# Key slices of the first two blocks stored from the query pool's tiles, x transposed in pairs, second context split sooner

## The chip, the core and the metric

The kernel runs on one core of one Trainium2 chip. The metric is the device time of one execution in microseconds. TensorE multiplies, ScalarE, VectorE and GpSimd do the elementwise work, SyncE issues nearly all DMA transfers. Each engine works through its own instructions in order and waits on semaphores for the others.

## The reference

The input `x` has 32 sequences of 100 tokens with 512 features. One layer is computed in float32: a cross-attention against a second input, the context, with a causal mask, and a mixture-of-experts feed-forward.

```python
q = (layernorm(x) @ WQ.T)      # 16 heads of 32
k = ctx @ WK.T
v = ctx @ WV.T
scores = q @ k.T / sqrt(32), causal mask     # per sequence and head
x = x + (softmax(scores) @ v) @ Wfc.T + bfc
h = layernorm(x)
# each of 16 experts picks 12 tokens of every sequence by its softmax score
x = x + sum over experts of gelu(h@Wg.T) * (h@Wu.T) @ Wd.T * weight + shared expert(h)
```

The mask lets a query see only keys up to its own position, so just the first 100 context tokens of each sequence take part.

## The kernel before

Every large product is computed from two parts of each operand. A helper copies a tile to a rounded high part on ScalarE (`split`, L101, or L135 in `ctx_split`) and subtracts it from the original on VectorE or GpSimd for the low part (L102, L136). `mm3` (L56) then issues three matmuls for each of four 128-feature slices: high by high, low by high, high by low. All projections go to PSUM tiles named `kv`, of which there are two (`pj=2`).

The 3200 context tokens are cut into nine blocks of two or three times 128 tokens (`KVB`). For each block, `kproj(j, c)` computes one of four key slices (`c`, 128 features), `kkeep` copies it to an SBUF tile `kk` on ScalarE (L204) and stores it to the DRAM tensor `kD` (L205). `vproj` and `vkeep` do the same for values (tile `vt`, two of them, L187, tensor `vD`). The pool of `kk` has two tiles of 384 columns, the pool of the query tiles `q` three of 400 columns:

```python
BUF = dict(cr=4, raw=6, cx=8, x=4, v=2, kk=2, kt=2, vt=2, q=3, p=5, pt=5, y=2, pj=2, sc=1, tr=2)
```

A tile of a pool can be written again only when everything that reads it, a DMA store included, is done. Keys come back from `kD` per unit of work (`kload`, L210). The x rows of a batch of four sequences are loaded (`x_load`), measured (`x_stats`: VectorE, then two small GpSimd instructions for `rs`, L152 and L153), normalized (`x_norm`, L159), and transposed by `x_turn`: four TensorE transposes (L171) into one of two PSUM tiles `ms`, then a ScalarE cast `xnh` (L101) and a VectorE subtract `xnl` (L102), which frees the `ms` tile. Queries come from `qproj` and `qkeep` (L230).

`prologue()` fills this pipeline. It handles context blocks 0 and 1 whole and prepares block 2; then the loop over 32 units (four feature slices for each of eight batches) runs scores (L240), softmax (L251 to L275), turned probabilities (L281, L286) and values (L296), with the remaining context blocks mixed in. After it come the feed-forward groups and the experts. In the prologue and the units the order of instructions on all engines is the order in which the code is written, so a line that stands earlier in `prologue()` is issued earlier on each engine that it uses. SyncE likewise issues the loads and stores in that order: the load of `x(1, 0)`, which reuses the tile of x block (0, 0), stands ahead of the store of the second value tile, the first key store of block 1, and `kload(0)`.

Of the kernel before, what the change touches and what calls it, by code (L numbers as in the profile page):

```python
# [7 lines left out]
F32 = mybir.dt.float32  # L8
# [13 lines left out]
SB = T // NSB  # L22
# [4 lines left out]
KMAX = 384  # L27
# [13 lines left out]
def f32(ap):  # L41
    return ap.bitcast(F32)
# [18 lines left out]
def attention(tc, K, F):  # L61
    nc = tc.nc
    with ExitStack() as ctx, ExitStack() as kvctx:
        def pool(name, bufs, stack=ctx, **kw):
            return stack.enter_context(tc.tile_pool(name=name, bufs=bufs, **kw))
# [4 lines left out]
        qp = pool("a_q", BUF["q"])  # L70
# [10 lines left out]
        kkp = pool("a_kk", BUF["kk"], kvctx, side="right")  # L81
# [22 lines left out]
        def load_w(w, dk):  # L104
            r = raw.tile([128, D], F32, name="raw")
            nc.sync.dma_start(r, K.wA[w, :, dk, :])
            return r

        def split_w(w, dk, r):
            split(WH[w][:, dk, :], WL[w][:, dk, :], r)  # L110

        def load_wc(w, c):
            r = raw.tile([128, D], F32, name="raw")
            nc.sync.dma_start(r.rearrange("p (d n) -> p d n", d=NC4),
                              K.wA[w, :, :, c * 128:(c + 1) * 128])
            return r

        def split_wc(w, c, r, eng=None):
            cs = slice(c * 128, (c + 1) * 128)
            split(WH[w][:, :, cs], WL[w][:, :, cs], r.rearrange("p (d n) -> p d n", d=NC4), eng)  # L120
# [3 lines left out]
        def ctx_load(j, d):  # L124
            t0, n = KSTART[j] * 128, KVB[j] * 128
            cr = crp.tile([128, KMAX], F32, name="cr")
            nc.sync.dma_start(cr[:, 0:n], K.ctxT[d, :, t0:t0 + n])
            cur["cr", j, d] = cr

        def ctx_split(j, d, eng=nc.gpsimd):  # L130
            n = KVB[j] * 128
            cr = cur.pop(("cr", j, d))
            h = cxp.tile([128, KMAX], FR, name="cxh")
            l = cxp.tile([128, KMAX], FR, name="cxl")
            nc.scalar.copy(h[:, 0:n], cr[:, 0:n])  # L135
            eng.tensor_tensor(l[:, 0:n], cr[:, 0:n], f32(h[:, 0:n]), ALU.subtract)  # L136
            cur.setdefault(("ch", j), []).append(h)
            cur.setdefault(("cl", j), []).append(l)

        def x_load(sb, b):  # L140
            xt = xp.tile([S, D], F32, name="xt")
            r0 = (sb * 4 + b) * S
            nc.sync.dma_start(xt, K.x[r0:r0 + S, :])
            cur["x", sb, b] = xt

        def x_stats(sb, b):
            st = stp.tile([S, 6], F32, name="bst")
            mv = stp.tile([S, 2], F32, name="mv")
            rs = stp.tile([S, 1], F32, name="rs")
            nc.vector.bn_stats(st, cur["x", sb, b])  # L150
            nc.vector.bn_aggr(mv, st)
            nc.gpsimd.tensor_scalar(rs, mv[:, 1:2], EPS, None, ALU.add)  # L152
            nc.gpsimd.tensor_tensor(rs, rs, K.nhalf[0:S, 0:1], ALU.pow)  # L153
            cur["mv", sb, b] = mv, rs

        def x_norm(sb, b):
            xt = cur["x", sb, b]
            mv, rs = cur["mv", sb, b]
            nc.vector.tensor_scalar(xt, xt, mv[:, 0:1], rs, ALU.subtract, ALU.mult)  # L159
# [16 lines left out]
        def vproj(j, i):  # L176
            ps = ps_kv.tile([128, D], F32, name="kv")
            cs = slice(i * 128, (i + 1) * 128)
            ch, cl = cur["ch", j], cur["cl", j]
            mm3(nc, ps, [((ch[d][:, cs], cl[d][:, cs]),  # L180
                          (WH[1][:, d, :], WL[1][:, d, :])) for d in range(NC4)],
                by_term=(j == 0))
            return ps

        def vkeep(j, i, ps):
            v = vtp.tile([128, D], F32, name="vt")
            nc.scalar.copy(v, ps)  # L187
            t0 = (KSTART[j] + i) * 128
            nc.sync.dma_start(K.vD[t0:t0 + 128, :], v)

        def kproj(j, c):
            n = KVB[j] * 128
            cs = slice(c * 128, (c + 1) * 128)
            ch, cl = cur["ch", j], cur["cl", j]
            pk = ps_kv.tile([128, D], F32, name="kv")
            mm3(nc, pk[:, 0:n], [((WH[0][:, d, cs], WL[0][:, d, cs]),
                                  (ch[d][:, 0:n], cl[d][:, 0:n])) for d in range(NC4)],
                by_term=(j == 0))
            return pk

        def kkeep(j, c, pk):
            t0, n = KSTART[j] * 128, KVB[j] * 128
            kk = kkp.tile([128, KMAX], F32, name="kk")
            nc.scalar.copy(kk[:, 0:n], pk[:, 0:n])  # L204
            nc.sync.dma_start(K.kD[:, c, t0:t0 + n], kk[:, 0:n])  # L205

        def kload(u):
            sb, c = divmod(u, NC4)
            kt = ktp.tile([128, SB], F32, name="kt")
            nc.sync.dma_start(kt, K.kD[:, c, sb * SB:(sb + 1) * SB])  # L210
            cur["k", u] = kt
# [99 lines left out]
        def prologue():  # L311
            nc.gpsimd.dma_start(mask, K.mask)
            z = stp.tile([128, 128], F32, name="zero")
            nc.vector.memset(z, 0.0)
            zp = ps_ms.tile([128, NC4, 128], F32, name="ms")
            for _ in range(WARM):
                nc.tensor.matmul(zp[:, 0, :], z, z, start=True, stop=True)
            wk = [load_wc(0, 0)]
            for d in range(NC4):
                ctx_load(0, d)  # L320
            wk += [load_wc(0, c) for c in range(1, NC4)]
            wv = [load_w(1, 0), load_w(1, 1)]
            split_wc(0, 0, wk[0])
            for d in range(NC4):
                ctx_split(0, d, nc.vector)
            wv.append(load_w(1, 2))
            for b in range(2):
                x_load(0, b)
            p0 = kproj(0, 0)
            split_wc(0, 1, wk[1])  # L330
            wv.append(load_w(1, 3))
            kkeep(0, 0, p0)
            p0 = kproj(0, 1)
            split_wc(0, 2, wk[2])
            split_wc(0, 3, wk[3])
            for b in range(2, 4):
                x_load(0, b)
            for d in range(NC4):
                ctx_load(1, d)
            wq = [load_wc(2, 0), load_wc(2, 1)]  # L340
            kkeep(0, 1, p0)
            p0 = kproj(0, 2)
            split_w(1, 0, wv[0])
            split_w(1, 1, wv[1])
            kkeep(0, 2, p0)
            p0 = kproj(0, 3)
            split_w(1, 2, wv[2])
            x_stats(0, 0)
            split_w(1, 3, wv[3])
            wq += [load_wc(2, 2), load_wc(2, 3)]  # L350
            kkeep(0, 3, p0)
            p0 = vproj(0, 0)
            x_norm(0, 0)
            x_stats(0, 1)
            x_stats(0, 2)
            x_norm(0, 1)
            x_stats(0, 3)
            for d in range(NC4):
                ctx_split(1, d, nc.vector)
            x_norm(0, 2)  # L360
            x_norm(0, 3)
            vkeep(0, 0, p0)
            p0 = vproj(0, 1)
            split_wc(2, 0, wq[0])
            for d in range(NC4):
                ctx_load(2, d)
            x_load(1, 0)
            vkeep(0, 1, p0)
            for c in range(NC4):
                kkeep(1, c, kproj(1, c))  # L370
                if c == 0:
                    for b in range(4):
                        x_turn(0, b)
                if c:
                    split_wc(2, c, wq[c], nc.gpsimd)
                    ctx_split(2, c - 1)
                else:
                    kload(0)
            x_load(1, 1)
            ctx_load(3, 0)  # L380
            x_stats(1, 0)
            vkeep(1, 0, vproj(1, 0))
            x_norm(1, 0)
# [153 lines left out]

        with tc.manual_schedule(engines={mybir.EngineType.Pool}):
            prologue()
            for u in range(NU - 3):  # L540
                sb, c = divmod(u, NC4)
# [3 lines left out]
                j, ck = divmod(u - KS, NC4)  # L545
# [784 lines left out]
```

## Time and profile before

| quantity | value |
|---|---|
| time, median of 3 runs | 1678.12 us (1677.43 to 1681.89) |
| profiled execution, its own time | 1681.51 us |
| profiled execution, span | 1679.6 us |
| mean granted TensorE clock | 0.997 |
| TensorE busy | 1660.7 us (99%) |
| ScalarE, VectorE, GpSimd busy | 679.2, 920.8, 625.2 us |
| mean DMA rate over the span | 141 GB/s |

A row of a profile view names the line of the code, the engine, the operation and `out<-in` by the program's tile names. "Idle before" is the time that the engine stood still just ahead of an instruction, with the instruction or transfer that ended it. The clock column is the share of full TensorE speed that was granted.

### The profile page before, as it was taken

The page shows a single profiled execution, that of the slowest core. Times are in us where ns is not written, and L with a number is a line of the kernel's source. Part 1 is how long each engine was busy: PE and PEld are TensorE (multiplying, and loading weights), DVE is VectorE, ACT ScalarE, POOL GpSimd, SP SyncE. Part 2 cuts the span into 40 slices and gives each one's busy share as a digit, 9 for nine tenths or more (in the row PEclk, how much of TensorE's full clock was granted, in tenths as well). Part 3 has the DMA queues.
Part 4 walks back from the last instruction along what each step waited for, and adds up shares of the span by engine and source line. Part 5 has one row for each costly group of instructions (what it writes and reads, how often), then busy time and mean ns, then how long its engine had stood idle before and what let it go on. Part 6 is the DMA issues. An engine that isn't in the chain of part 4 may idle for free.

```text
span 1679.6 us, 28091 instructions
## 1 busy us (share of the span) xinstructions
PE 1660.7 (99%) x10879; PEld 1526.4 (91%) x10879; DVE 920.8 (55%) x2199; ACT 679.2 (40%) x1088; POOL 625.2 (37%) x542
## 2 busy tenths in 40 slices
PE   8999999999999999999999999999999999999998
PEld 7998888879889898989899999999999999999998
DVE  4778777665433434343555555555555555555542
ACT  4556555553111111112334444444444444444442
POOL 2778777680110011010243344333344333344011
PEclk9999999999999999999999999999999999999999
DMA  7456554556312223211445554455555455555452
GB/s 214 145 171 189 159 159 142 172 191 196 103 66 90 76 82 132 82 44 42 144 163 152 166 169 145 157 161 146 166 167 151 155 161 155 159 161 159 136 165 63
DMA packets 107126, 237.47 MB, mean 141 GB/s; under 512 B 14162, under 2 KB 58419, under 8 KB 106993
## 3 DMA queue, kind: packets, MB, share of 16 engines
q1 hardware_dynamic: 93632, 209.99, 38.3%
q0 software_dynamic: 12944, 25.22, 7.9%
q8 instruction: 85, 1.39, 0.3%
q10 hardware_dynamic: 416, 0.48, 0.1%
q14 instruction: 49, 0.39, 0.1%
HBM read 181.90 MB, written 53.73 MB: 140 GB/s over the span
## 4 chain that ended last, share of the span: by engine, by line
PE 93%; DVE 2%; ACT 1%; POOL 1%; DMA 1%; issue 1%; SPq 0%; ACTq 0%; POOLq 0%; DVEq 0%
PE gu L56 49%; PE dn L56 24%; PE kv L56 10%; PE m L56 3%; PE ms L281 2%; PE ms L296 2%; POOL p L260 1%; PE sc L240 1%; DVE p L251 1%; DMA kD<-kk 1%; ACT pt L286 1%; PE ms L171 0%; DVE y L102 0%; PE m L1109 0%; DMA raw<-wA 0%
## 5 line engine op out<-in xcount | busy, mean ns | idle before, releaser
L56 PE MATMUL gu<-xh,whl 128*128 128x384 f32 (+1 forms) x3200 | 642.5, 332 | 0.0
L56 PEld LDWEIGHTS gu<-xh,whl 128*128 128x128 f32 x3200 | 556.5, 188 | 20.0 <-issue 1.3
L56 PE MATMUL dn<-whl,hh 128*128 128x512 f32 x1168 | 365.9, 394 | 0.0
L740 DVE TENSOR_TENSOR whl<-wraw,whl 128x1536 fp32r<-128x1536 f32 x142 | 249.7, 1759 | 203.2 <-ACT whl L739 181.6
L945 POOL DMA_INDIRECT gx<-xnD,iq x180 | 226.8, 1260 | 359.9 <-DVE big L976 300.3
L56 PE MATMUL gu<-xl,whl 128*128 128x384 f32 (+1 forms) x1600 | 336.7, 332 | 0.0
L56 PEld LDWEIGHTS gu<-xl,whl 128*128 128x128 f32 x1600 | 279.9, 188 | 0.0
L774 ACT CAST hh<-g 128x384 fp32r<-128x384 f32 (+1 forms) x200 | 100.9, 505 | 408.8 <-DVE g L771 380.4
L771 DVE TENSOR_TENSOR g<-g,gu 128x384 f32<-128x384 f32 (+1 forms) x200 | 108.3, 542 | 255.5 <-PE gu L56 249.1
L56 PEld LDWEIGHTS dn<-whl,hh 128*128 128x128 f32 x1168 | 215.6, 188 | 35.8
L739 ACT CAST whl<-wraw 128x1536 fp32r<-128x1536 f32 x142 | 210.0, 1479 | 61.8 <-PE dn L56 58.7
L56 PE MATMUL dn<-whl,hl 128*128 128x512 f32 x584 | 230.6, 395 | 0.0
L770 ACT ACTIVATE g<-gu 128x384 f32<-128x384 f32 (+1 forms) x200 | 96.3, 482 | 237.6 <-PE gu L56 236.9
L775 DVE TENSOR_TENSOR hl<-g,hh 128x384 fp32r<-128x384 f32 (+1 forms) x200 | 113.3, 566 | 114.2 <-ACT hh L774 113.7
L988 POOL DMA_INDIRECT out_dram<-x,isl x48 | 77.8, 1620 | 171.3 <-ACT x L987 161.5
L56 PEld LDWEIGHTS dn<-whl,hl 128*128 128x128 f32 x584 | 109.7, 188 | 25.2
L260 POOL TENSOR_TENSOR p<-p,mx 100x800 f32<-100x800 f32 x64 | 96.7, 1531 | 64.4 <-DVE mx L251 61.4
L275 POOL TENSOR_TENSOR p<-p,sm 100x800 f32<-100x800 f32 x64 | 100.9, 1577 | 5.8 <-DVE sm L270 3.6
L251 DVE CUSTOM_DVE_ANT_0 p<-sc,mask 100x100 f32<-100x100 f32 x512 | 95.4, 256 | 0.0
L1025 POOL TENSOR_TENSOR x<-x,bfc 128x512 f32<-128x512 f32 x23 | 30.9, 1369 | 154.2 <-DMA x<-x 154.2
L977 ACT CAST xh<-big 128x512 fp32r<-128x512 f32 x59 | 36.6, 621 | 101.6 <-DVE big L976 101.6
L269 DVE TENSOR_REDUCE sm<-p 100x8 f32<-100x800 f32 x64 | 63.1, 986 | 24.6 <-ACT p L264 24.6
(160 smaller groups left out, 1645.1 us busy)
## 6 DMA issues: line engine op xcount, KB each, us to landing
wraw<-wE SPq DMA_DIRECT2D x144, 768.0 KB
yD<-y SPq DMA_DIRECT2D x31, 400.0 KB
xt<-x SPq DMA_DIRECT2D x32, 200.0 KB
vD<-vt SPq DMA_DIRECT2D x25, 256.0 KB
kt<-kD SPq DMA_DIRECT2D x32, 200.0 KB
v<-vD SPq DMA_DIRECT2D x8, 800.0 KB
xnD<-xn SPq DMA_DIRECT2D x25, 256.0 KB
out_dram<-x SPq DMA_DIRECT2D x25, 256.0 KB
```

What stands on the lines that cost most here:

```text
L56: r = nc.tensor.matmul(out, t[0][a], t[1][b], start=(first and i == 0), stop=(last and i == n - 1))
L251: nc.vector.tensor_tensor_reduce(out=p[:, bb, h, :], in0=sc[:, h, cs], in1=mask, scale=ISCALE, scalar=NEG, op0=ALU.add, op1=ALU.max, accum ...
L260: nc.gpsimd.tensor_tensor(pv, pv, mx[:, :, None].to_broadcast([S, 8, S]), ALU.subtract)
L275: nc.gpsimd.tensor_tensor(pv, pv, sm[:, :, None].to_broadcast([S, 8, S]), ALU.mult)
L739: nc.scalar.copy(h, r)
L740: nc.vector.tensor_tensor(l, r, f32(h), ALU.subtract)
L770: nc.scalar.activation(g[:, 0:t], pg[:, 0:t], AF.Gelu)
L771: nc.vector.tensor_tensor(g[:, 0:t], g[:, 0:t], pu[:, 0:t], ALU.mult)
L774: nc.scalar.copy(hh[:, 0:t], g[:, 0:t])
L775: nc.vector.tensor_tensor(hl[:, 0:t], g[:, 0:t], f32(hh[:, 0:t]), ALU.subtract)
L945: nc.gpsimd.indirect_dma_start(out=g[:, k, :], out_offset=None, in_=self.K.xn.rearrange("t (a f) -> (t a) f", f=128), in_offset=bass.Indir ...
L988: ins = nc.gpsimd.indirect_dma_start(out=self.K.out, out_offset=bass.IndirectOffsetOnAxis(ap=r.isl[:, i:i + 1], axis=0), in_=o, in_offset= ...
```

## The change

Three edits, all in the attention's start. First, `kkeep` takes its tile from the query pool for the third and fourth key slice of blocks 0 and 1. Second, the four `x_turn` calls of the first batch, which followed the first key slice of block 1 together, are issued two after the second slice and two after the third. Third, in `prologue()` the four splits of context block 1 move ahead of the norm of x block 1 and of the statistics of x blocks 2 and 3.

```diff
         def kkeep(j, c, pk):
             t0, n = KSTART[j] * 128, KVB[j] * 128
-            kk = kkp.tile([128, KMAX], F32, name="kk")
+            if j < 2 and c > 1:
+                kk = qp.tile([128, SB], F32, name="q")
+            else:
+                kk = kkp.tile([128, KMAX], F32, name="kk")
             nc.scalar.copy(kk[:, 0:n], pk[:, 0:n])
             nc.sync.dma_start(K.kD[:, c, t0:t0 + n], kk[:, 0:n])
...
             p0 = vproj(0, 0)
             x_norm(0, 0)
             x_stats(0, 1)
-            x_stats(0, 2)
-            x_norm(0, 1)
-            x_stats(0, 3)
             for d in range(NC4):
                 ctx_split(1, d, nc.vector)
+            x_norm(0, 1)
+            x_stats(0, 2)
+            x_stats(0, 3)
             x_norm(0, 2)
             x_norm(0, 3)
             vkeep(0, 0, p0)
...
             for c in range(NC4):
                 kkeep(1, c, kproj(1, c))
-                if c == 0:
-                    for b in range(4):
+                if c in (1, 2):
+                    for b in (2 * c - 2, 2 * c - 1):
                         x_turn(0, b)
                 if c:
                     split_wc(2, c, wq[c], nc.gpsimd)
```

## The prediction

> **What bounds the kernel now.** I read the page first (engines and slices), then who waits for whom on TensorE, then TensorE and ScalarE in order of time for 15 to 43 us, the chain of waits there, and the windows with the granted clock. The page says that TensorE is the bound; only its idle time or slow clock can be won.
>
> ```profile
> PE 1660.7 (99%) x10879; PEld 1526.4 (91%) x10879; DVE 920.8 (55%) x2199; ACT 679.2 (40%) x1088; POOL 625.2 (37%) x542
> ```
>
> TensorE's waits in the first 400 us, in the form "waiter <- releaser: us in total, times, longest":
>
> ```profile
> PE ms L296 <- ACT pt L286: 3.3, 4, 2.3
> PE kv L56 <- ACT kk L204: 3.1, 2, 2.0
> PE ms L281 <- ACT pt L286: 2.0, 2, 1.6
> ...
> PE ms L171 <- DVE xnl L102: 0.8, 1, 0.8
> ```
>
> The second and last row lie in the prologue, which the change edits. TensorE and then ScalarE in order of time (start, us, instruction, idle before it and its releaser):
>
> ```profile
> 16.63 0.49 PE L56 MATMUL kv<-wh,cxh 128*128 128x512 f32 x1 [1.16 <-ACT kk L204]
> ...
> 21.98 0.50 PE L56 MATMUL kv<-wh,cxh 128*128 128x512 f32 x1 [1.96 <-ACT kk L204]
> ...
> 29.54 1.05 PE L171 MATMUL ms<-ident,xt 100*128 100x100 f32 x8 [0.85 <-DVE xnl L102]
> ...
> 34.76 1.09 PE L56 MATMUL kv<-wh,cxh 128*128 128x512 f32 x4
> ```
> ```profile
> 16.20 0.37 ACT L204 COPY kk<-kv 128x256 f32<-128x256 f32 x1 [2.77 <-DMA kD<-kk]
> ...
> 21.56 0.37 ACT L204 COPY kk<-kv 128x256 f32<-128x256 f32 x1 [3.94 <-DMA kD<-kk]
> ```
>
> ScalarE can't copy the third key slice out of PSUM before the first one's store has left its `kk` tile, nor the fourth before the second's. The PSUM tiles `kv` number two, so TensorE stops at the first value projection until the third slice is out (16.63) and at the second until the fourth is out (21.98). The chain of waits has the two stores:
>
> ```profile
> 10.06 6.04 DMA kD<-kk
> ...
> 17.16 4.30 DMA kD<-kk
> ```
>
> The stops also cost clock. Windows of 2 us: TensorE busy after the first comma; the granted clock, the DMA share and GB/s are the last three numbers.
>
> ```profile
> 20.00:22.00 2.00, 0.04 (x2) 0.02 (x1) 1.91 (x4) 0.44 (x2) 0.43 (x2) 1.00 1.01 298
> 22.00:24.00 2.00, 2.00 (x8) 1.65 (x9) 1.75 (x5) 2.00 (x6) 1.44 (x4) 0.87 0.35 110
> 24.00:26.00 2.00, 2.00 (x6) 1.56 (x5) 2.00 (x7) 0.16 (x1) 0.77 (x2) 0.50 0.69 213
> 26.00:28.00 2.00, 2.00 (x15) 1.98 (x14) 0.61 (x2) 0.59 (x1) 0.00 (x0) 0.78 0.91 292
> 28.00:30.00 2.00, 1.15 (x13) 0.87 (x10) 1.06 (x2) 1.19 (x3) 0.00 (x0) 1.00 0.31 75
> 30.00:32.00 2.00, 2.00 (x19) 1.98 (x18) 1.33 (x3) 0.98 (x2) 0.00 (x0) 1.00 0.71 244
> ```
>
> From 0.87, 0.50 and 0.78 the clock was halved for 0.52 + 2.00 + 0.88 = 3.4 us, from 23.48 to 26.88, after 2.1 us without matmuls.
>
> **The change part by part.** My measure is the start of the block-1 value projection `vproj(1, 0)`, 34.76 before: from there TensorE runs without a gap over 0.2 us up to 168 us.
>
> *Key slices in `q` tiles.* Four copies and four stores stay what they are (copy 0.37 us, 128 KB); only the tile is another. The first and second slices of block 0 keep `kk`. In the forecast the third copy follows its projection. The row of matmuls of 256 columns has a pitch of 0.12 us and starts its last one at 15.19; the third slice's last one is 12 matmuls earlier, 13.75, and ends 0.28 later at 14.03, so the copy runs 14.1 to 14.5 instead of 16.20. Then ScalarE casts the third and fourth value-weight quarter. The fourth lands at 15.77 (the trace's completion events), so its cast ends at 16.4 and the fourth slice's copy at 16.7 instead of 21.9. TensorE: `vproj(0, 0)` starts at 15.31, one pitch after 15.19, and takes 12 x 0.2325 = 2.79 (its quarters are split by 15.7 and 17.1, needed at 16.9 and 17.6); `vproj(0, 1)` from 18.1 to 20.9, since its PSUM tile is free from 16.7.
>
> *Second context split sooner.* No instruction is added. The context quarters land at 18.4 to 19.6 and ScalarE's casts, no longer behind the fourth copy, end at 20.0. VectorE's four subtracts at 0.42 then end at 20.7. In the old order two statistics (0.69 + 0.18 each) and a norm (0.55) stand before them; these now come after, so the norms of x blocks 1, 2 and 3 end near 21.2, 23.4 and 24.3. Cover: TensorE's transposes of them come at 24.1, 25.9 and 26.2. If it were gone, they would cost their excess, at most the 2.3 us that were moved. GpSimd's order is the same; between the small rs steps and its first weight part it sat idle 8.25 us (25 to 33).
> `kproj(1, 0)` can then start at 20.9: the first value copy frees its PSUM tile at 20.5, the low context parts are there at 20.7. Each key projection of block 1 takes 12 x 0.12 = 1.44.
>
> *Turns two by two.* Sixteen transposes, four casts and four subtracts stay. Before, the third turn waits 0.85 for the `ms` tile that the first turn's subtract frees. Now `kproj(1, 2)` (1.44) stands between the pairs and covers 24.4 to 25.9; the two subtracts end at 25.35 and 25.85, so the third turn waits for nothing. Two more changes between matmuls and transposes: nothing if as smooth as elsewhere, 0.1 each at worst. On ScalarE the second key copy passes the first pair of casts, and the third copy, one query-weight cast and one context cast the second pair, which makes GpSimd's split of that weight earlier.
> Sum: `kproj(1, 0)` 20.9, `kproj(1, 1)` 22.3, two turns 23.7 (0.35 each), `kproj(1, 2)` 24.4, two turns 25.9, `kproj(1, 3)` 26.6, `vproj(1, 0)` **28.0**. Gain 34.76 - 28.0 = **6.7 us**: half-speed work 3.4/2 = 1.7, gaps 1.16 + 1.96 + 0.85 = 4.0, and 1.0 of starts after stops and smaller waits.
>
> *SyncE and what is late next.* SyncE issues in order, and each DMA here also waits until the one eight before it has landed. The load of `x(1, 0)` waits for the first turn, now behind `kproj(1, 1)`: 24.3 instead of 28.38. Queued behind it are a value store, the store of key slice (1, 0) and then `kload(0)`, which waits for that store. From the old landings (3.1 us for the store, 2.5 for the load) the store lands near 28.3 and the keys near 31; the scores need them at 42.88 - 6.7 = 36.1. GpSimd starts its weight parts at 25.6 instead of 33.10 and is done with the last context slice near 36.5, needed at 40. The x norm of the next batch ends at 33.9, needed at 35.7. So the gain stays.
>
> *The `q` ring.* The four stores take slots 1, 2, 3, 1; the queries' first three copies then wait for three of those stores. Their price is nothing to the end of a store: the nearest row is the wait removed, 3.94. I take 0: the first two stores land near 22, the others near 32 and 33, and the first three query copies come at 33, 40 and 47.
>
> *Rule against trace, twice.* The clock was full at 28 to 34 although 27.84 to 30.36 held almost nothing but transposes and a wait. The Trainium skill (TensorE: Matmul & The Clock Gate, Part 4: PE-mode transpose) says that transposes do not count as busy the same way. By it a half-clock stretch would follow that block and the splitting would save 1.7 more (8.4 in sum); by the trace it saves none, and I take the trace.
> The same page (Part 1: The HAM clock gate) lets the clock fall after at least one idle window of about 3.4 us, in free-running windows. The row 24 to 26 has 0.50 after a stop of 2.1 us. By the page the stop cost no clock, and only 6.7 - 1.7 = 5.0 could be gained; by the trace 6.7. That the windows run free does matter: whether a stop of 2 us halves the clock can differ between executions.
>
> **From the profiled execution to the median.** Its span is 1679.6, its time 1681.51, 1.9 around it; that is 3.4 above the median of 1678.12. It has a second such stretch far from the change:
>
> ```profile
> 352.00:354.00 2.00, 0.10 (x1) 0.00 (x0) 1.19 (x3) 1.21 (x3) 1.36 (x2) 1.00 1.05 367
> 354.00:356.00 2.00, 1.60 (x33) 1.31 (x34) 1.93 (x4) 1.23 (x3) 1.86 (x2) 0.64 1.04 319
> 356.00:358.00 2.00, 2.00 (x32) 1.67 (x35) 0.99 (x2) 1.06 (x3) 0.89 (x1) 0.50 0.45 173
> ```
>
> Two stretches at 1.7 are just the 3.4, so the median run may have had neither. On the profiled execution I forecast 1681.5 - 6.7 = 1674.8. On the median the gain is 5.0 if the early stretch was absent, 6.7 if present; at 6 to 4 that is 5.7: 1678.1 - 5.7 = **1672.4**.
>
> **The rivals.** *A, the waits go and nothing takes their place:* 1671.4 to 1673.1, chance 0.60. For it: every deadline above has over 1 us of room but the PSUM tile at 20.5 and the context at 20.7, against 20.9.
> *B, a smaller gain:* 0.30. DMA is at 0.86 to 1.08 of its share from 14 to 22 us, so the context quarters (18.4 to 19.6) have no reserve. If they or the fourth value quarter land 1 to 3 us later, TensorE stops again just before `kproj(1, 0)`: gain 2 to 4, 1674 to 1676. The late stretch, missing in the median run but present after, does the same: 5.0 - 1.7 = 3.3, 1674.8.
> *C, slower:* 0.07. The stores of block 1's keys stay stuck on SyncE behind `x(1, 0)`, the value store and `kload(0)`; the second query copy then waits for a `q` slot and ScalarE blocks with it, as it did for `kk`. It costs from the point where that store lands after 40 us, eats the gain at 46, and is over 0.3% slower when it lands after 51; I give it 1684. Against it: the slowest store of the trace took 6.04 us at a full DMA, and after 23 us DMA is half empty.
> *D, nothing:* 0.03. If the first value projection waited for something else at 16.63, the time would be 1678. Against it, the copy before it ends at 16.57.
>
> **How the numbers follow.** About 0.3% (5.0 us, to 1673.1 or 1683.2) is what a measurement of this kernel can tell from no change. A is faster (0.60), B and D are the same (0.33), C is slower (0.07). The range leaves out C and the ends: from 1669.5 (A with 8.4, by the transposes' rule) to 1677.0 (B with a gain of 1). The likeliest case alone is 1671.4 to 1673.1.
>
> **What would show it.** Right: no wait of TensorE on a key copy, none of L171 on VectorE, `vproj(1, 0)` near 28, the clock at 1.00 from 14 to 350, keys' first load landed before 36. Wrong: a new TensorE gap at 20 to 21 (context or PSUM tile late), a half-clock stretch at 20 to 28, or a ScalarE query copy waiting for a key store.

## The result, and the profile after

The changed kernel takes 1676.09 us (median; 1673.05 to 1681.3) against 1679.45 for the kernel before in the same comparison: ratio 0.9982, 95% interval 0.9974 to 0.9989. A second comparison gave 1674.98 against 1680.06, ratio 0.9972 (0.9962 to 0.9982). So there is a gain of 3.4 to 5.1 us, and it is real, but it is smaller than the 5.7 us of the forecast of 1672.4, and stays under the 0.3% that the forecast named as what can be told from no change. The profiled execution has a span of 1674.0 and a time of 1675.84 (forecast for it: 1674.8), against 1679.6 and 1681.51.

The engines' line of the page after the change:

```profile
PE 1657.8 (99%) x10879; PEld 1523.1 (91%) x10879; DVE 917.9 (55%) x2199; ACT 679.3 (41%) x1088; POOL 625.7 (37%) x542
```

TensorE still bounds it. Its busy time fell by 2.9 with the same number of instructions, and its idle time from 18.9 to 16.2 (span less busy time). The 2.9 is mostly the one profile: two more of the kernel before (below) are busy for 1658.3 and 1657.5, two more of the kernel after for 1657.2 and 1657.6. On the averages of three, idle time falls from 18.9 to 14.8 and busy time from 1658.8 to 1657.5, so most of the gain is removed waiting. Who TensorE waits for in the first 100 us after the change (waiter <- releaser: us in total, times, longest):

```profile
...
PE ms L284 <- ACT pt L289: 0.8, 1, 0.8
PE kv L56 <- DVE wl L102: 0.4, 2, 0.2
PE kv L56 <- ACT q L207: 0.4, 1, 0.4
PE kv L56 <- ACT wh L101: 0.4, 2, 0.2
```

The 3.1 us on the key copies are down to one wait of 0.4, and the row of `ms L171` on VectorE is gone. What is new is the first row: the turn of the softmax's probabilities (line 284) waits for ScalarE's copy of earlier ones out of PSUM. Lines behind the edited function are three higher than before. TensorE in order of time:

```profile
13.41 0.50 PE L56 MATMUL kv<-wh,cxh 128*128 128x512 f32 x1 [0.40 <-ACT q L207]
...
17.24 0.40 PE L56 MATMUL kv<-wh,cxh 128*128 128x512 f32 x1
...
25.11 0.85 PE L171 MATMUL ms<-ident,xt 100*128 100x100 f32 x8
...
27.25 1.09 PE L56 MATMUL kv<-wh,cxh 128*128 128x512 f32 x4
...
35.37 0.96 PE L243 MATMUL sc<-kt,q 32*100 32x100 f32 x32
...
51.21 0.87 PE L284 MATMUL ms<-ident,p 100*100 100x100 f32 x8 [0.81 <-ACT pt L289]
```

`vproj(0, 0)` and `vproj(0, 1)` start at 13.41 and 17.24 instead of 16.63 and 21.98, and `vproj(1, 0)` at 27.25 instead of 34.76. That is 7.5 us, more than the forecast 6.7. At the end of the span 5.6 are left, and in the medians fewer. So the question is where a gain that was there at 27 us went. The windows of the stretch that the change aimed at (TensorE busy after the first comma; clock, DMA share and GB/s last) show no gap and the full clock:

```profile
20.00:22.00 2.00, 2.00 (x17) 2.00 (x17) 1.92 (x5) 1.23 (x3) 0.64 (x2) 1.00 1.00 294
22.00:24.00 2.00, 2.00 (x21) 2.00 (x20) 1.35 (x3) 0.94 (x4) 1.08 (x3) 1.00 0.99 313
24.00:26.00 2.00, 2.00 (x21) 2.00 (x20) 1.31 (x3) 1.65 (x5) 1.01 (x1) 1.00 0.89 212
```

Now follow the new wait back. VectorE after the change, and then SyncE's issues:

```profile
32.81 0.55 DVE L159 TENSOR_SCALAR xt<-xt,mv,rs 100x512 f32<-100x512 f32 x1 [3.43 <-POOL rs L153]
35.15 0.69 DVE L150 BATCH_NORM_STATS2 bst<-xt 100x6 f32<-100x512 f32 x1 [1.79 <-DMA xt<-x]
...
37.06 1.23 DVE L159 TENSOR_SCALAR xt<-xt,mv,rs 100x512 f32<-100x512 f32 x1 [1.00 <-POOL rs L153]
...
38.70 0.25 DVE L254 CUSTOM_DVE_ANT_0 p<-sc,mask 100x100 f32<-100x100 f32 x1
```
```profile
24.33 0.38 SPq L208 DMA_DIRECT2D kD<-kk  x1
29.46 0.32 SPq L213 DMA_DIRECT2D kt<-kD  x1
29.88 0.39 SPq L208 DMA_DIRECT2D kD<-kk  x1
30.35 0.90 SPq L208 DMA_DIRECT2D kD<-q  x2
31.36 0.32 SPq L143 DMA_DIRECT2D xt<-x  x1
```

The load `kload(0)` (L213) reads keys that the store at 24.33 is still writing. SyncE's row of waits has it as `SPq L213 <- DMA kD<-kk: 4.7, 1, 4.7`. Behind it in the queue stand three key stores and the load of `x(1, 1)` (the last row). In the kernel before, the same chain was there: that x load went out at 36.11, and VectorE came to its statistics at 41.15 without waiting. SyncE and VectorE before:

```profile
36.11 0.32 SPq L143 DMA_DIRECT2D xt<-x  x1
```
```profile
41.15 0.69 DVE L150 BATCH_NORM_STATS2 bst<-xt 100x6 f32<-100x512 f32 x1
...
44.67 0.24 DVE L251 CUSTOM_DVE_ANT_0 p<-sc,mask 100x100 f32<-100x100 f32 x1
```

The change brought TensorE forward by 7.5 us and this load by 4.75 only (5.9 and 4.3 on the averages of three profiles of each kernel). VectorE, which works in order, waits 1.79 for it and another 1.00 for GpSimd's `rs`, and the first softmax maxima stand behind both: 38.70, which is 3.34 after the first scores (35.37). The 1.00 was there before the change too; the 1.79 is new. Before, the maxima came 1.79 after the scores (the same figure as the wait by chance). The late maxima put GpSimd's softmax steps back, ScalarE's exponentials follow, and at 51.21 TensorE stops for 0.81.

### The profile page after: what moved, and what is told of

The parts are those of the page before. It is cut to its first block, busy times and chain, and to the rows that moved or that the text cites. A ratio compares the mean times of both kernels' runs of the same rounds, so it can differ in the third digit from the quotient of the medians.

```text
span 1674.0 us, 28093 instructions
## 1 busy us (share of the span) xinstructions
PE 1657.8 (99%) x10879; PEld 1523.1 (91%) x10879; DVE 917.9 (55%) x2199; ACT 679.3 (41%) x1088; POOL 625.7 (37%) x542
## 4 chain that ended last, share of the span: by engine, by line
PE 92%; POOL 2%; DVE 2%; ACT 1%; issue 1%; DMA 1%; SPq 0%; POOLq 0%; ACTq 0%; DVEq 0%
PE gu L56 49%; PE dn L56 24%; PE kv L56 10%; PE m L56 3%; PE ms L284 2%; POOL p L263 2%; PE ms L299 2%; PE sc L243 1%; DVE p L254 1%; ACT pt L289 1%; DMA raw<-wA 1%; PE ms L171 0%; DVE y L102 0%; PE m L1112 0%; PE m L968 0%
## 5 line engine op out<-in xcount | busy, mean ns | idle before, releaser
L56 PEld LDWEIGHTS dn<-whl,hh 128*128 128x128 f32 x1168 | 215.5, 188 | 36.1 <-ACT hh L777 0.4
```

Source lines behind the costliest of these rows:

```text
L56: r = nc.tensor.matmul(out, t[0][a], t[1][b], start=(first and i == 0), stop=(last and i == n - 1))
```

## The experiments

Four explanations were open. The gain is given back at the load of `x(1, 1)`, behind `kload(0)`. Or edits 2 and 3 (context split sooner, turns two by two) bring nothing and edit 1 is all there is. Or the half-speed stretch was worth less than the 1.7 us put on it. Or the profiled execution of before was unusual, so that its 34.76 was a bad place to count from.

The starts that the text refers to, one profile in each row, in us. "Maxima" are the first softmax maxima on VectorE; "third turn" is TensorE's third group of turned probabilities.

| kernel | vproj(0,0) | vproj(0,1) | vproj(1,0) | first scores | maxima (after scores) | third turn | span |
|---|---|---|---|---|---|---|---|
| before | 16.63 | 21.98 | 34.76 | 42.88 | 44.67 (1.79) | 65.24 | 1679.6 |
| before, 2nd profile | 16.35 | 21.66 | 32.86 | 40.98 | 42.77 (1.79) | 63.37 | 1676.1 |
| before, 3rd profile | 17.38 | 22.63 | 33.85 | 41.97 | 43.76 (1.79) | 64.33 | 1677.4 |
| after | 13.41 | 17.24 | 27.25 | 35.37 | 38.70 (3.34) | 59.15 | 1674.0 |
| after, 2nd profile | 14.60 | 18.07 | 28.24 | 36.36 | 39.49 (3.13) | 59.94 | 1671.7 |
| after, 3rd profile | 15.61 | 18.35 | 28.25 | 36.37 | 39.09 (2.73) | 59.53 | 1671.3 |
| edit 1 alone | 13.47 | 17.77 | 29.79 | 37.90 | 39.69 (1.78) | 60.28 | 1674.8 |
| edits 2 and 3 alone | 17.52 | 22.66 | 33.46 | 41.83 | 44.16 (2.33) | 64.60 | 1677.9 |
| keys' load later | 14.39 | 19.20 | 29.16 | 37.27 | 39.26 (1.98) | 59.69 | 1673.1 |
| keys' load later, again | 13.13 | 17.25 | 27.16 | 35.28 | 36.59 (1.31) | 57.66 | 1672.1 |
| edit 1, keys' load later | 14.42 | 19.13 | 31.16 | 39.28 | 41.07 (1.79) | 61.65 | 1674.5 |
| keys' load later, value weights first | 13.65 | 16.40 | 28.50 | 36.62 | 37.94 (1.31) | 59.02 | 1673.8 |
| fillers | 17.18 | 24.70 | 35.88 | 44.00 | 45.79 (1.79) | 66.40 | 1679.2 |

The steadiest number in it is the time from `vproj(1, 0)` to the third turn. It is 30.5 us in nine of the thirteen profiles, whenever TensorE gets there: in all three of before, and in every variant with edit 1 alone, the fillers or the keys' load later. In the three profiles of the whole change it is 31.9, 31.7 and 31.3. So the loss sits in this stretch, and it is 1.4, 1.2 and 0.8 us. (Edits 2 and 3 alone have 31.1, from another wait: there the norm of `x(1, 0)` waits 4.45 for GpSimd's `rs`.)

### Edit 1 alone: the `q` tiles, in the old order

```diff
-            kk = kkp.tile([128, KMAX], F32, name="kk")
+            if j < 2 and c > 1:
+                kk = qp.tile([128, SB], F32, name="q")
+            else:
+                kk = kkp.tile([128, KMAX], F32, name="kk")
```

> Edit 1 alone: the third and fourth key slices leave through q tiles, the order of the x turns and of the context splits is the old one. Theory W (the change's gain is its removed waits, and part of it is given back behind the load of the first keys): the two waits on key copies are gone, but VectorE's low context parts come behind two statistics and a norm (about 2.3 us), so TensorE waits some 1.3 us at the block-1 key projection, and 0.85 us at the third turn as before. vproj(1, 0) starts near 29.5 instead of 27.25 with the whole change; time about 1.5 to 2 us above the whole change, 1.5 to 2 us below before. Rival T (edit 1 carries everything, the two reorderings are idle): same time as the whole change, 1676.1. Rival R (the reordering carries the gain): no change against before, 1679.5.

Measured: 1676.07 against 1680.06, ratio 0.9978 (0.9971 to 0.9984), between the two ratios of the whole change. By the time it was rival T that came true; theory W had it 1.5 to 2 us slower. In its trace the turns still stand together, and the third waits:

```profile
24.57 1.04 PE L171 MATMUL ms<-ident,xt 100*128 100x100 f32 x8 [0.85 <-DVE xnl L102]
...
29.79 1.09 PE L56 MATMUL kv<-wh,cxh 128*128 128x512 f32 x4
```

`vproj(1, 0)` is 2.5 us later than in the whole change, 0.5 of it there at `vproj(0, 1)` already, so edits 2 and 3 do what they were made for. But the maxima are only 1.0 later (39.69 against 38.70) and the third turn 1.1 (60.28 against 59.15): with edit 1 alone VectorE's statistics of `x(1, 1)` start at 36.17 without a wait. Of the 2.5 us that edits 2 and 3 win, some 1.4 are lost again on the x load.

### Edits 2 and 3 alone

```diff
             x_stats(0, 1)
-            x_stats(0, 2)
-            x_norm(0, 1)
-            x_stats(0, 3)
             for d in range(NC4):
                 ctx_split(1, d, nc.vector)
+            x_norm(0, 1)
+            x_stats(0, 2)
+            x_stats(0, 3)
...
-                if c == 0:
-                    for b in range(4):
+                if c in (1, 2):
+                    for b in (2 * c - 2, 2 * c - 1):
                         x_turn(0, b)
```

> Edits 2 and 3 alone: the kk pool still carries all key slices, the turns go two by two and context 1 is split sooner. Theory W: the 1.2 and 2.0 us waits on key copies stay, since the fourth key slice still waits for the store of the second; only the 0.85 us wait at the third turn goes. Time 0.5 to 1.2 us below before. Rival R: most of the 3.4 us of the whole change.

Measured: 1679.75, ratio 1.0000 (0.9991 to 1.0008), so not the 0.5 to 1.2 us that were expected. Its TensorE rows:

```profile
17.52 0.50 PE L56 MATMUL kv<-wh,cxh 128*128 128x512 f32 x1 [4.11 <-ACT kk L204]
...
22.66 0.50 PE L56 MATMUL kv<-wh,cxh 128*128 128x512 f32 x1 [0.55 <-ACT kk L204]
...
33.46 1.19 PE L56 MATMUL kv<-wh,cxh 128*128 128x512 f32 x4 [0.62 <-ACT kk L204]
```

The waits on the key stores stay, and there is a third one: with block 1's keys in two tiles as well, `vproj(1, 0)` has to wait for a key copy. It starts at 33.46, within the 32.86 to 34.76 of the three profiles of before. Without free tiles the better order brings nothing that can be measured.

### The keys' load behind the load of `x(1, 1)`

The whole change, with `kload(0)` moved past the loop and the x load. Nothing else differs.

```diff
                 if c:
                     split_wc(2, c, wq[c], nc.gpsimd)
                     ctx_split(2, c - 1)
-                else:
-                    kload(0)
             x_load(1, 1)
+            kload(0)
```

> The whole change, with kload(0) issued behind the load of x(1, 1) instead of ahead of three key stores and that load. Theory W: SyncE no longer stands still for the first key store's landing (4.7 us in the profile of the changed kernel) with the load of x(1, 1) behind it; that load lands 3 us sooner, VectorE has no wait on it (1.79 us), the first maxima start over 1.5 us sooner, and TensorE's wait of 0.81 us at 51 us goes. Time about 1 us below the whole change: 1675.1, and 4.4 us below before. Rival L (the keys then come too late for the first scores at 35.4): the same or up to 1 us slower than the whole change, with a wait of L243 on the kt load. Rival N (the wait at 51 us costs nothing in the median): 1676.1.

Measured: 1674.96 against 1680.06, ratio 0.9969 (0.9958 to 0.9980). It was run once more beside the unchanged kernel after:

> The whole change with the first key load behind the load of x(1, 1), once more, in one job with the changed kernel. Theory W: 1.0 to 1.5 us below the changed kernel (0.8 to 1.1 seen at the wait near 51 us), ratio to before 0.997. Rival N: no difference to it.

> The changed kernel as it is, timed beside the next three. Theory W: about 1676.1 and a ratio of 0.998 to before, as in the first result; its VectorE starts the first maxima about 3.2 us after the first scores' start (1.79 in the kernels before).

Measured: 1673.99, ratio 0.9965 (0.9953 to 0.9977), against 1674.98, 0.9972 (0.9962 to 0.9982), for the kernel after. The trace of the second run can be laid beside that of the kernel after, since `vproj(1, 0)` starts within 0.1 us of it (27.16 and 27.25). SyncE and VectorE:

```profile
28.22 0.31 SPq L143 DMA_DIRECT2D xt<-x  x1
29.28 0.32 SPq L213 DMA_DIRECT2D kt<-kD  x1
```
```profile
32.98 0.69 DVE L150 BATCH_NORM_STATS2 bst<-xt 100x6 f32<-100x512 f32 x1
...
34.89 1.22 DVE L159 TENSOR_SCALAR xt<-xt,mv,rs 100x512 f32<-100x512 f32 x1 [1.00 <-POOL rs L153]
...
36.59 0.25 DVE L254 CUSTOM_DVE_ANT_0 p<-sc,mask 100x100 f32<-100x100 f32 x1
```

The x load goes out 3.1 us earlier, and the keys' load no later than before the move (29.28 against 29.46), since the store that it waits for is the same. The DMA engines, which stood nearly empty behind the blocked queue, have work: their share from 28 to 30 us is 0.59 instead of 0.12. VectorE's 1.79 us are gone, and the maxima come at 36.59, 1.31 after the scores. GpSimd's first softmax step (line 263) starts at 38.20 instead of 40.31, and the exponential ahead of the probabilities' copies at 48.22 instead of 49.81. TensorE has no wait at the turns, and its third turn comes at 57.66 instead of 59.15. That is 1.5, or 1.4 after the 0.1 at the start: 0.8 of it the wait, the rest smaller delays. In the medians it is 1.0, with intervals that overlap: the cause of the wait is shown, its worth in the median is near what can be told apart. Both runs of this version have a lower ratio than any other that was run, by less than the intervals' width.

### Edit 1 alone, with the keys' load later

If edits 2 and 3 are worth something once the x load is out of the way, leaving them out of the version above should cost it.

> Edit 1 alone, with the first key load behind the load of x(1, 1). Theory W says that the two reorderings (edits 2 and 3) bring TensorE some 2 us ahead, and that the late x(1, 1) takes this back on VectorE; edit 1 alone never gets so far ahead that x(1, 1) is late. Then this kernel is no faster than edit 1 alone (1676.1, within 0.5 us), and the whole change with the same later key load beats it by 1 us or more. Rival K (the later key load is worth 1 us by itself, whatever the order): 1675, the same as the whole change with it.

Measured: 1675.33, ratio 0.9974 (0.9964 to 0.9984), 1.3 us above the version with all edits in the same comparison (theory W expected 1 us or more). In the traces `vproj(1, 0)` is 4.0 and the third turn 4.0 later (61.65 against 57.66). Some of that is the execution and not the order: `vproj(0, 1)` is already 1.9 later, because the third slice's copy and the last value-weight quarter came later. What is left, 2.1, is the turns' wait and the context. So nothing of the edits' gain is given back any more, but by the medians alone it is not shown that they help: the intervals overlap.

### The fourth value-weight quarter ahead of the x loads

The version above, with the load of that quarter moved ahead of the first two x loads, since `vproj(0, 0)` waits for it in several of the traces.

```diff
-            for b in range(2):
-                x_load(0, b)
...
             wv.append(load_w(1, 3))
+            for b in range(2):
+                x_load(0, b)
...
-            x_stats(0, 0)
             split_w(1, 3, wv[3])
+            x_stats(0, 0)
```

> The whole change with the later key load, and the fourth value-weight load issued ahead of the first two loads of x (their statistics behind its split). Theory W: with the waits on key copies gone, the prologue is bound by landings; the fourth value-weight quarter lands 1 to 1.5 us sooner, TensorE's waits of 0.2 to 1.2 us on its high and low part go, and the time falls by 0.3 to 1 us below the same kernel without it. Rival D (the context quarters, which land at 18 to 19.6 whatever the order, bind right behind): no difference.

Measured: 1674.97, ratio 0.9973 (0.9963 to 0.9983), no better than without. `vproj(0, 1)` does start earlier, at 16.40, but then:

```profile
20.53 0.74 PE L56 MATMUL kv<-cxh,wh 128*128 128x256 f32 x4 [1.25 <-ACT vt L187]
...
22.69 0.74 PE L56 MATMUL kv<-cxh,wh 128*128 128x256 f32 x4 [0.46 <-ACT vt L187]
```

The value copies stand on ScalarE behind the casts of block 1's context, which had waited for their data (3.65 on `cr<-ctxT`). Here the next transfer binds: with the DMA share at 0.84 to 1.09 from 14 to 20 us, moving one load forward moved the stop.

### Fillers in the second stop

Nine matmuls on zeros behind `vproj(0, 0)`, in the kernel before. They were to keep TensorE busy through the second stop, so that the clock would stay up while the stop itself stayed, and so to price the half-speed stretch.

```diff
             p0 = vproj(0, 0)
+            for _ in range(FILL):
+                nc.tensor.matmul(zp[:, 0, :], z, z, start=True, stop=True)
```

> The kernel before, with nine more matmuls of zeros (0.21 us each, into the warm-up's PSUM tile, read by nobody) behind the first value projection: they fill the second wait of TensorE (1.96 us) and change no wait. This measures the clock's part of the forecast by itself. Theory H (the half-clock stretch at 23 to 27 us is there in most executions): the time falls by 1.0 to 1.7 us, and the mean granted clock of its runs lies 0.001 above that of before. Rival U (the stretch is there only in some executions, such as the profiled one): under 0.6 us, and the same mean clock in most runs.

Measured: 1681.19, ratio 1.0008 (1.0001 to 1.0014), slower by 1.1 us. In its trace the first stop took 3.71 us and no second one followed: the fillers pushed `vproj(0, 1)` to 24.70. They filled a stop that wasn't there, and this run doesn't price the clock. But why was there no second stop?

### More profiles of the kernel before and the kernel after

> The kernel before, unchanged, one look. Theory P (the profiled execution that the forecast rests on was not the usual one: its clock was halved at 9.8 to 13.2 us, so TensorE came late to the first wait): here TensorE is at the first wait sooner, near 13.3, the wait on the third key copy is about 3.5 to 4 us instead of 1.16, the one on the fourth about 0.5 instead of 1.96, and the second value projection starts near 22, as in the profile. Theory Q (the profiled execution was the usual one): 1.2 and 2.0 us again, and a half-clock stretch from about 23.5.

> The kernel before, unchanged, a second look. Theory P: as in the first one, waits of about 4 and 0.5 us; where the half-clock stretch falls may differ. Theory Q: 1.2 and 2.0 us.

> The changed kernel, unchanged, one more look. Theory W: a wait on the load of x(1, 1) on VectorE between 1 and 4 us and a TensorE wait of 0.5 to 1.5 us at the second pair of turned probabilities near 51 us. Rival N: no wait there; the one in the first profile was an accident.

Measured, one time each: 1677.99 and 1679.27 for the kernel before, 1673.51 for the kernel after. The third profile of after is that of its timed run above. The two waits on the key copies in the two new profiles of before, two rows each:

```profile
16.35 0.50 PE L56 MATMUL kv<-wh,cxh 128*128 128x512 f32 x1 [2.29 <-ACT kk L204]
...
21.66 0.50 PE L56 MATMUL kv<-wh,cxh 128*128 128x512 f32 x1 [0.69 <-ACT kk L204]
```
```profile
17.38 0.80 PE L56 MATMUL kv<-wh,cxh 128*128 128x512 f32 x1 [4.24 <-ACT kk L204]
...
22.63 0.50 PE L56 MATMUL kv<-wh,cxh 128*128 128x512 f32 x1 [0.19 <-ACT kk L204]
```

The starts differ little from the first profile (16.63 and 21.98), since the stores set them, but the stop moves from the second to the first projection. TensorE came to the first wait at 14.06 and 13.14 (start less wait) instead of 15.47, and so waited longer there; that is theory P. Windows of the second profile of before:

```profile
16.00:18.00 2.00, 1.65 (x6) 1.32 (x7) 1.15 (x2) 1.34 (x3) 0.00 (x0) 0.82 0.87 242
18.00:20.00 2.00, 2.00 (x6) 1.54 (x5) 1.17 (x4) 0.00 (x0) 1.17 (x2) 0.50 1.09 316
...
22.00:24.00 2.00, 2.00 (x10) 1.66 (x9) 1.85 (x5) 1.83 (x5) 1.35 (x5) 1.00 0.29 91
```

Here the clock is halved at 17.3 to 20.7, so that `vproj(0, 0)` runs slowly into a stop that it would have stood out anyway: the fourth key store ends it at 21.66 as before. From 22 on the clock is full, and `vproj(1, 0)` comes at 32.86, 1.9 earlier than in the first profile. In these profiles a half-speed stretch ahead of the second stop costs little of the time, and the one behind it 1.6 us: from `vproj(0, 1)` to `vproj(1, 0)` it takes 12.8 us in the first profile and 11.2 in both others. The profile that the prediction counted from had it behind.

## Why the prediction was right and wrong

**Key slices in `q` tiles: right.** The slices are copied to `q` tiles at 12.99 and 15.79, forecast 14.1 and some 16.3, and the projections follow. Edit 1 alone has the whole measurable gain.

**Second context split, turns two by two: right in place.** No gap at 20 to 21, no wait of the turns, and `vproj(1, 0)` at 27.25, 28.24 and 28.25 in three profiles against 28.0. The edits' effect up to there came as worked out.

**The `q` ring at 0: right.** The first and third query copies after the change (32.40 and 47.64) wait for their matmuls and for no store, and the second (38.79) comes 8 us after the last of these stores was issued.

**The clock of the stop: right in size, and a matter of chance.** The prediction put 1.7 on the half-speed stretch and gave it 4 in 10 for the median run. Of three profiles of before, one has it where it costs, and there it is worth 1.6 (12.8 less 11.2). That the profile at hand was this one was chance. On average `vproj(1, 0)` starts at 33.8 before and 27.9 after, a gain of 5.9 against the 5.7 forecast for the median run. The 6.7 was counted from the first profile, where the pair of first profiles gives 7.5. (The stop ahead of the stretch is 1.96 us by its row, not 2.1.)

**Turns and the clock: right to leave the saving out.** With edit 1 alone the four turns stand together at 22.86 to 25.4, with a wait of 0.85 in them, and every window of its trace from 22 to 32 has the clock at 1.00. Grouped transposes cost no clock here.

**"SyncE and what is late next ... So the gain stays": failed.** The prediction followed `kload(0)` to its own deadline (forecast 31, needed 36.1) and `x(1, 0)` to its norm, and both held: the first key store landed at 29.4 instead of 28.3, and the keys still came in time. Its size was off, though: 5.1 us for that store (24.33 to 29.4) and not the 3.1 of before; and the DMA engines are not half empty there after the change, as rival C's counter-argument had it (0.99, 0.89 and 0.82 from 22 to 28 us). And it didn't follow what is queued behind `kload(0)`. Three key stores were named in rival C, but the load of `x(1, 1)` right after them was not, nor VectorE's statistics of it ahead of the first maxima. At the third turn that costs 1.1 of 5.9 on the averages of the three profiles (64.3 to 59.5 is 4.8), and 1.4 in the pair of traces with the same start. So rival C had the right mechanism, a queue stuck behind the keys' load, on the wrong consumer: not ScalarE and a `q` slot, but VectorE and an x block, at 1 us instead of some 12 (1684 against 1672.4).

**From the profile to the median.** The forecast was made against 1678.12, the median of three runs. The larger samples have 1679.45 and 1680.06. Of the 3.7 us between 1672.4 and 1676.09, 1.3 is this reference and 2.3 is a smaller gain (3.4 for 5.7). The x load explains 1.1 of the 2.3. The 4.6 that are then to be expected lie in the interval of the second comparison (3.0 to 6.4 us, measured 5.1) and just above that of the first (1.8 to 4.4). The two intervals overlap, and what made the first one smaller isn't settled. What came true is the smaller gain of rival B, by neither of its causes as far as the profiles show. TensorE did wait for the casts of value-weight quarters (L101), but 0.4, 0.8 and 0.6 us in the three profiles, and the gain at `vproj(1, 0)` was there all the same. The late stretch at half clock stood in one profile of three, after the change as before it; for the timed runs it isn't known.

## What to carry to other kernels

When a change brings one engine forward, list everything that stands in the issuing queue behind each load that waits for a store, and give each its new deadline; the load that waits may be in time while the one behind it is late. Edits that remove a stop are worth what is left at the next stage that works in order, so look for a row that moves less than its consumer (here 4.75 us against 7.5). In a stretch bound by transfers, take two or three profiles before putting a price on a stop or on a clock stretch, and search them for two instructions that lie equally far apart in each, as the 30.5 us here: a loss of 1 us shows against that.

## What the runs showed of the hardware

Stores of 128 KB to DRAM took 6.04 and 4.30 us in the kernel before (issued at 10.06 and 17.16, DMA share 0.86 to 1.08 from 10 to 22 us), about 3.1 at 29.2, and 5.1 in the kernel after (issued at 24.33). The load that waits for such a store stops all of SyncE's queue: 2.7 us before, 4.7 after the change.

The stretches of half clock, each 3.4 us or twice that, stood at different places in each profile of one kernel: at 9.8, 23.5 and 354.6 in the first of before, at 17.3 in the second, at 15.0 to 21.8 in the third; at 350.2 in the first of after and at 8.6 in the second. Besides, TensorE begins at half clock, and for how long differs. The clock column doesn't show this, for it prints 1.00 where the profile has no record yet, but the matmuls do: those of 256 columns start 0.21 us apart at half speed and 0.12 at full. The half speed lasts to about 6.4 us in the first profile of before, to 10.4 in the second, and to 13.7 in the third of after. Before the change the first wait on a key copy takes up such a late start. After it there is little left to do so, and the two profiles of after whose clock was halved ahead of `vproj(0, 0)` start `vproj(1, 0)` 1.0 us later than the one whose clock wasn't; with three profiles this is a likely cause and not a shown one.

Five of the thirteen profiles have a half-clock stretch between 346 and 358 us, far behind the edits. From the third turn to the end of the span these take 1614.4 to 1614.9 us, and the eight others 1611.8 to 1613.4. The averages differ by 1.9, near the 1.7 that 3.4 us at half speed lose.

The kernel's scatter goes with the clock: in the first and largest sample of before beside the experiments (51 runs), those at a mean granted clock of 0.997, 0.998 and 0.999 had medians of 1680.88, 1680.06 and 1679.15, close to 1 us for each 0.001. The change raises the mean over all runs for which it is on record from 0.998 to 0.999, so about 1 us of its gain goes with a steadier clock; that was not tested by itself.
